# Softmax block factors of a perceiver layer: turned once a sequence and spread by DMA instead of widened and transposed for every block

## The chip, the cores and the metric

The kernel runs on one core of a Trainium2 chip. A core has five engines with a queue each: TensorE (PE, with its weight loads shown as PEld), VectorE (DVE), ScalarE (ACT), GpSimd (POOL) and SyncE (SP, which issues most DMAs here). Each queue is worked off in order, and engines wait for each other through semaphores. The metric is the device time of one execution in microseconds (us).

## The reference, cut to what matters

A layer of three parts over 16 sequences of 128 rows by 512 in float32: cross attention to a context of 2048 rows a sequence (16 heads of 32), a Mamba block with an MLP, and a gated expert layer. The change touches the attention's softmax and some instructions beside it:

```
q, k, v = heads(layernorm(x) @ wq.T + bq), heads(ctx @ wk.T + bk), heads(ctx @ wv.T + bv)
attn = softmax(q @ k.T * 32 ** -0.5)          # over 2048 columns of the context
x = x + (attn @ v) @ wo.T + bo
x_dbl = silu(conv(x_part)) @ x_proj_w.T       # 1024 -> 32 + 16 + 16 (dt, B, C)
dt = softplus(x_dbl[:32] @ dt_proj_w.T + b)   # then a scan over the rows
```

## The kernel before, in words

The context of a sequence is worked off in SB = 4 blocks of 512 rows. A block's softmax uses the block's own maxima; the four results are joined at the end with a factor for each row, block and head: the exponential of block maximum less overall maximum, over the joined sum. These factors are in `stats[b]`, 128 rows by 4 x 16.

The main loop runs over units u. In the first NU = 256 units, each does one group of four heads of one block: `scores` (L302) of the four heads into banks[0] to banks[3] of PSUM, `maxima` (L310, DVE), `exps` (L320, ACT), then four turns: turn i transposes columns i of all four heads' exponentials (L333) into a bank, and a copy to the tile pT frees it (L338 on ACT; L336 on DVE for turn 2, except in the first three units of a sequence, where ACT does all four). In the next unit `weighted` (L346) multiplies them with v. So a sequence b takes 16 units, from 16b on, and its end is called e = 16b + 16. Beside this, a unit holds

- the keys and values of the next blocks in a Strassen-like scheme of seven products (L240, into pa and pc), whose differences of context tiles t1 to t4 POOL makes (`ctx_sums`, L232) in every fourth unit, and whose sums are made on DVE and ACT (`k_sum` L260 and L258, `v_sum` L270 and L268),
- the Mamba part of earlier sequences, two at a time: `decays` (L665, ACT), `scan` (L679 and L682, DVE) and sums on POOL (`inputs` L644, ysum L695), from unit 54 on; `dt_third` (L632 to L635, POOL) makes dt and dx for four units each,
- and what the tables put in: functions are filed by unit under late, after, inner, middle, loads, head and behind, each table having a fixed place in the loop's body. `late` functions take a PSUM bank of their own; turn 3 then comes after them.

After NU the units hold the MLP and experts (`feed`) beside the remaining scans.

At the end of a sequence: `joined` (head of e) gathers the maxima (four copies, L422), `joined_first` (inner of e), `shares` and `joined_second` (e+1) and `joined_third` (head of e+2, L447) make the factors. `spread_out` (POOL, L453) repeats each factor over the 32 columns of its head in a tile fx. `scaled`, late in e+3 for block 0 and in e+4 for blocks 1 to 3, transposes fx with four transposes (L459) into a bank and multiplies the block's result avs by it, L464 for block 0 and L466 for the others, and POOL sums up (L467). `attended` (e+6, L472) takes the sum.

Further names: `turned` (L389, copy L391) transposes the normalized queries in unit 16b - 6; `x_proj` (L581, copy L584) is late in every unit 18 of 32, with a weight tile of 64 columns; `dt_first` (L611, L618), `dt_second` (L625) and `silu_second` (L570) are DVE and PE work of the Mamba part. SP issues the context tiles (L154), the rows B and C spread over all partitions (`load_bc`, L593) and weights.

Of the kernel before, what the change touches and what calls it, by code (L numbers as in the profile page):

```python
# [8 lines left out]
FP = mybir.dt.float32  # L9
AF = mybir.ActivationFunctionType  # L10
ALU = mybir.AluOpType
# [4 lines left out]
P = 128  # L16
B, NQ, D, S = 16, 128, 512, 2048
H, HD = 16, 32
KC = D // P
SB = S // 512  # L20
DI, DS, DTR = 1024, 16, 32
EC = DI // P
# [3 lines left out]
GT = GB * NQ  # L26
# [8 lines left out]
def perceiver_layer(ctx: ExitStack, tc: tile.TileContext, a: dict, out: bass.AP):  # L35
    nc = tc.nc
# [18 lines left out]
    x1d = dram.tile([B, NQ, D], FP, tag="x1d", name="x1d")  # L55
    zd = [dram.tile([NQ, D], FP, tag=f"zd{b}", name=f"zd{b}") for b in range(B)]
    xnd = [dram.tile([NQ, D], FP, tag=f"xnd{b}", name=f"xnd{b}") for b in range(B)]
    bcd = [dram.tile([2 * DS, GT], FP, tag=f"bcd{g}", name=f"bcd{g}") for g in range(B // GB)]

    mv = const.tile([P, B, 2], FP, tag="mv", name="mv")  # L60
# [48 lines left out]
    with ExitStack() as es:  # L109
# [8 lines left out]
        def acon_in(name, shape, src=None):  # L118
            t = acon.tile(shape, FP, tag=name, name=name)
            nc.gpsimd.dma_start(t, a[name] if src is None else src)  # L120
            return t
# [19 lines left out]
        def heads(ps):  # L141
            return ps.rearrange("p (k q) -> p k q", q=P)
# [171 lines left out]
        def exps(u):  # L314
            b, sb, hg = split(u)
            nm, sm = stats[b]
            pr = pool.tile([P, 4, 512], FP, tag="pr", name=f"pr{u}", bufs=1)
            for j in range(4):
                h = hg * 4 + j
                nc.scalar.activation(  # L320
                    pr[:, j, :],
                    banks[j],
                    AF.Exp,
                    bias=nm[j][:, sb, hg : hg + 1],
                    accum_out=sm[:, sb, h : h + 1],
                )
            prs[u] = pr
# [89 lines left out]
        def joined(b):  # L417

            parts, sm = stats[b]
            nm = keep.tile([P, SB, H], FP, tag="nm", name=f"nm{b}")  # L420
            for j in range(4):
                nc.vector.tensor_copy(  # L422
                    nm.rearrange("p s (k j) -> p s k j", j=4)[:, :, :, j], parts[j]
                )
            stats[b] = nm, sm
# [18 lines left out]
        def joined_third(b):  # L444
            nm, sm, lo, flat = stats[b]
            stats[b] = nm
            nc.vector.tensor_tensor(nm, nm, lo.to_broadcast([P, SB, H]), ALU.mult)  # L447

        fxs = {}

        def spread_out(b, sb):
            fx = keep.tile([P, H, HD], FP, tag="fx", name="fx", bufs=3)
            nc.gpsimd.tensor_copy(fx, stats[b][:, sb, :].unsqueeze(2).to_broadcast([P, H, HD]))  # L453
            fxs[b, sb] = fx.rearrange("p h d -> p (h d)")

        def scaled(b, sb, ps):
            fx = fxs.pop((b, sb))
            for hg in range(4):
                nc.tensor.transpose(heads(ps)[:, hg, :], fx[:, hg * P : (hg + 1) * P], ident)  # L459
            t = avs.pop((b, sb))  # L460
            if sb == 0:
                aT = keep.tile([P, KC, P], FP, tag="aT", name="aT", bufs=1)
                avs[b] = aT
                nc.vector.tensor_tensor(aT, t, heads(ps), ALU.mult)  # L464
            else:
                nc.vector.tensor_tensor(t, t, heads(ps), ALU.mult)  # L466
                nc.gpsimd.tensor_tensor(avs[b], avs[b], t, ALU.add)  # L467

        def out_proj(aT, b, ps):
# [10 lines left out]
            moments_of(b)  # L480


        xproj = acon_in("xproj", [P, EC, DTR + 2 * DS])
        convw = acon_in("convw", [P, EC, 4])
        convb = acon_in("convb", [P, EC])
        dtb = acon_in("dtb", [P, EC])
# [89 lines left out]
            sgs.clear()  # L576

        def x_proj(g, ps):
            ps = ps[0 : DTR + 2 * DS, 0:GT]
            for ec in range(EC):  # L580
                nc.tensor.matmul(  # L581
                    ps, xproj[:, ec, :], xas[g, ec], start=(ec == 0), stop=(ec == EC - 1)
                )
            nc.vector.tensor_copy(xd[0 : DTR + 2 * DS, :], ps)  # L584
            nc.sync.dma_start(bcd[g], xd[DTR : DTR + 2 * DS, :])

        def load_bc(t, base):

# [41 lines left out]
        def dt_third(g, ec):  # L630
            dt, e, u = dts[g, ec]
            nc.gpsimd.tensor_tensor(dt, dt, e, ALU.subtract)  # L632
            nc.gpsimd.tensor_tensor(dt, dt, u, ALU.add)
            dx = ssm.tile([P, GT], FP, tag="dx", name="dx")
            nc.gpsimd.tensor_tensor(dx, dt, xas[g, ec], ALU.mult)  # L635
            dts[g, ec] = dt, dx
# [111 lines left out]
        def flat(ps):  # L748
            return ps.rearrange("p k q -> p (k q)")
# [3 lines left out]
        def bank():  # L753
            return free_banks.pop(0)

        def give_back(*ps):
            free_banks.extend(ps)
# [379 lines left out]
            )  # L1137


        early = {}  # L1140
        late, after, inner, middle, loads, head, behind = ({} for _ in range(7))

        def put(where, u, f):
            where.setdefault(u, []).append(f)

        for b in range(B):
            s = 16 * b
            if b:
                put(loads, s - 8, lambda b=b: load_x(b))
                put(loads, s - 5, lambda b=b: load_w(0, b))  # L1150
                put(inner, s - 8, lambda b=b: moments_of(b))
                put(middle, s - 7, lambda b=b: root_of(b))
                put(inner, s - 7, lambda b=b: normal(b))
                put(late, s - 4, lambda ps, b=b: queries(b, ps))
            e = s + 16
            put(loads, e + 5, lambda b=b: load_w(3, b))
            put(head, e, lambda b=b: joined(b))
            put(inner, e, lambda b=b: joined_first(b))
            put(middle, e + 1, lambda b=b: shares(b))
            put(inner, e + 1, lambda b=b: joined_second(b))  # L1160
            put(head, e + 2, lambda b=b: joined_third(b))
            for sb in range(SB):
                put(inner, e + 2 + (sb > 0), lambda b=b, sb=sb: spread_out(b, sb))
                put(late, e + 3 + (sb > 0), lambda ps, b=b, sb=sb: scaled(b, sb, ps))
            put(late, e + 6, lambda ps, b=b: attended(b, ps))
            put(middle, e + 7, lambda b=b: root_of(b))
            put(inner, e + 7, lambda b=b: normed(b))
            put(late, e + 8, lambda ps, b=b: z_turned(b, ps))
        for g in range(NG):
            p = 32 * (g + 1)  # L1170
            for ec in range(EC):
                put(loads, p + 8 + ec, lambda g=g, ec=ec: load_win(g, ec))
                put(loads, p + 8 + ec, lambda g=g, ec=ec: load_win(g, EC + ec))
                put(late, p + 9 + ec, lambda ps, g=g, ec=ec: x_part(g, ec, ps))
                put(late, p + 9 + ec, lambda ps, g=g, ec=ec: z_part(g, ec, ps))
                put(after, p + 10 + ec, lambda g=g, ec=ec: silu_first(g, ec, xas))
                put(after, p + Z_GATES[ec], lambda g=g, ec=ec: silu_first(g, ec, zss))
            put(late, p + 18, lambda ps, g=g: x_proj(g, ps))
            s = p + LAG
            for ec in range(EC):  # L1180
                put(loads, s - 4 + 4 * ec, lambda ec=ec: load_dtproj(ec))
                put(behind, s - 3 + 4 * ec, lambda ps, g=g, ec=ec: dt_first(g, ec, ps))
                put(middle, s - 2 + 4 * ec, lambda g=g, ec=ec: dt_second(g, ec))
                put(inner, s - 2 + 4 * ec, lambda g=g, ec=ec: dt_third(g, ec))
            for i in range(GB):
                for ec in range(WS):
                    put(loads, s + 32 + 2 * i, lambda g=g, i=i, ec=ec: load_wout(g, i, ec))
                put(loads, s + 31 + 2 * i, lambda b=g * GB + i: reload_x(b))
                put(late, s + 33 + 2 * i, lambda ps, g=g, i=i: projected(g, i, ps))
# [68 lines left out]
        ps = banks[2]  # L1258
# [8 lines left out]
        for u in range(last):  # L1267
            live = u < NU
# [39 lines left out]
                x_products(of, made, phase, pa, pc)  # L1308
            if live:
                exps(u)  # L1310
            if makes and u % 4 == 1:
                ctx_sums(made, ("t1", "t2"))
            if 0 <= u + 1 - 32 - LAG < 32 * NG:
                inputs(*divmod(u + 1 - 32 - LAG, 32))
            if makes and u % 4 == 1:
                ctx_sums(made, ("t3", "t4"))
            silu_third()
            if scans:
# [12 lines left out]
            if live and after_turns:  # L1331
                if u % 4 == 0:
                    places = [flat(avp), *places[:-1]]
                elif u % 2 and makes and u not in behind:
                    places[-1] = flat(pc)
            taken = sum(any(p is b for b in banks) for p in places)
            if live:
                for i in range(3 if taken else 4):
# [103 lines left out]
```

## Time and profile before

| what | value |
|---|---|
| median of 3 runs | 3791.14 us (3790.33 to 3794.2) |
| the profiled execution | 3793.75 us, span 3792.0 us, granted clock 0.996 |
| L459, transposes of fx | 256 matmuls, median 273 ns each |
| L464, L466, products with the factors | 16 + 48, 673 to 687 ns |
| L453, the widened factors on POOL | 64, 599 to 621 ns |
| L581, x_proj | 128 matmul records, weight load of 64 columns 137 ns |
| bc to landing | 512 DMAs of 512 KB, median 4.3 us |

A matmul's duration is its latency; matmuls follow each other faster than that. Rows of the timeline give the start in us, the duration in us, the engine, the line, the operation, the tiles written and read, the shapes and the count merged in the row; in brackets stands the idle time before it and what ended it. A unit is measured from its first L302 to that of the next unit. The middle batches repeat themselves within some hundredths of a us, with a period of 32 units.

### The profile page before, as it was taken

What the parts mean: (1) busy time and instruction counts of PE and PEld (TensorE: products, weight loads), DVE (VectorE), ACT (ScalarE), POOL (GpSimd) and SP (SyncE); (2) the same over time, 40 slices, a digit from 0 to 9 for tenths busy, and PEclk for the clock granted to TensorE, in tenths of its full rate; (3) what the DMA queues carried; (4) which work ended last, traced back from release to release, by engine and by line L of the source; (5) the groups of instructions that cost most, each with busy time, mean ns of one, the idle gap of its engine ahead of it and who ended that gap; (6) DMA issues with size and microseconds to landing.
All of it is one profiled execution on the core that took longest, in us unless ns stands there. A gap on an engine that the chain in (4) does not pass through costs nothing.

```text
span 3792.0 us, 70325 instructions
## 1 busy us (share of the span) xinstructions
PE 3742.2 (99%) x26120; PEld 2853.8 (75%) x26120; DVE 2689.9 (71%) x4853; ACT 2443.5 (64%) x5848; POOL 2109.4 (56%) x1969
## 2 busy tenths in 40 slices
PE   9999999999999999999999999999999999999999
PEld 7878887778777877787788878787878776655555
DVE  3444445887778777877788778877887777778843
ACT  3555556777767776777677767776777675544421
POOL 2111213675657666765666566766675667667720
PEclk9999999999999999999999999999999999999999
DMA  3111122444444435453534453445444558577752
GB/s 102 34 40 43 49 72 80 132 149 145 141 159 145 154 117 174 136 159 111 184 130 145 131 191 119 148 134 171 140 156 132 165 174 290 197 276 246 266 174 73
DMA packets 343223, 548.40 MB, mean 145 GB/s; under 512 B 24368, under 2 KB 227408, under 8 KB 342624
## 3 DMA queue, kind: packets, MB, share of 16 engines
q1 hardware_dynamic: 342432, 543.27, 43.2%
q8 instruction: 206, 3.38, 0.4%
q14 instruction: 137, 1.12, 0.1%
q0 software_dynamic: 448, 0.63, 0.1%
HBM read 527.29 MB, written 16.52 MB: 143 GB/s over the span
## 4 chain that ended last, share of the span: by engine, by line
PE 89%; DVE 5%; ACT 3%; DMA 1%; issue 1%; POOL 1%; SPq 0%; DVEq 0%; POOLq 0%; ACTq 0%
PE pa L240 24%; PE pc L240 17%; PE bank L333 11%; PE bank L302 7%; PE avp L346 6%; PE bank L527 5%; PE bank L1029 2%; PE bank L934 2%; PE bank L472 2%; PE bank L708 2%; PE bank L903 1%; PE avp L399 1%; PE pc L708 1%; PE avp L934 1%; PE pa L934 1%
## 5 line engine op out<-in xcount | busy, mean ns | idle before, releaser
L310 DVE TENSOR_REDUCE nm<-bank 128x1 f32<-128x512 f32 x1024 | 635.2, 682 | 249.2 <-PE bank L302 249.0
L695 POOL TENSOR_TENSOR ysum<-ysum,w 128x512 f32<-128x512 f32 x384 | 500.0, 1302 | 481.9 <-DVE hst L658 312.7
L320 ACT ACTIVATE pr<-bank,nm 128x512 f32<-128x512 f32 x1024 | 689.7, 687 | 96.0 <-DVE nm L310 92.0
L644 POOL TENSOR_TENSOR w<-dx,bc 128x512 f32<-128x512 f32 x512 | 653.8, 1298 | 4.6
L679 DVE TENSOR_TENSOR_SCAN hst<-hst,w 128x512 f32<-128x512 f32 x459 | 560.7, 1222 | 15.8 <-ACT hst L665 9.3
L338 ACT COPY pT<-bank 128x512 f32<-128x512 f32 x816 | 434.8, 585 | 180.8 <-PE bank L333 177.1
L665 ACT ACTIVATE hst<-dt,alog 128x254 f32<-128x254 f32 x918 | 439.2, 478 | 148.5 <-DVE hst L658 133.0
L333 PE MATMUL bank<-ident,pr 128*128 128x128 f32 x4096 | 514.3, 274 | 7.2 <-ACT pT L338 3.3
L333 PEld LDWEIGHTS bank<-ident,pr 128*128 128x128 f32 x4096 | 469.6, 141 | 57.5 <-issue 13.8
L346 PEld LDWEIGHTS avp<-pT,v 128*32 128x32 f32 x8192 | 208.6, 110 | 194.6 <-issue 176.7
L682 DVE TENSOR_TENSOR w<-hst,bc 128x512 f32<-128x512 f32 x459 | 317.4, 692 | 26.0 <-DMA bc<-bcd 10.4
L232 POOL TENSOR_TENSOR t<-c,c 128x512 f32<-128x512 f32 x128 | 164.0, 1281 | 260.0 <-PE pc L240 255.9
L302 PE MATMUL bank<-kt,qT 32*128 32x512 f32 x2048 | 300.9, 642 | 0.5 <-ACT pT L338 0.5
L346 PE MATMUL avp<-pT,v 128*32 128x128 f32 x8192 | 277.6, 276 | 0.0
L240 PE MATMUL pa<-t,ks 128*128 128x256 f32 x1024 | 249.9, 387 | 6.2 <-POOL t L232 6.2
L240 PE MATMUL pa<-vs,t 128*128 128x256 f32 x1008 | 244.7, 386 | 0.0
L240 PEld LDWEIGHTS pa<-t,ks 128*128 128x128 f32 x1024 | 184.9, 190 | 44.2 <-issue 10.6
L240 PEld LDWEIGHTS pa<-vs,t 128*128 128x128 f32 x1008 | 185.5, 190 | 34.6 <-issue 10.1
L320 ACT ACTIVATION_READ_ACCUMULATOR pr<-bank,nm 128x1 f32 x1024 | 209.8, 205 | 0.0
L336 DVE COPY pT<-bank 128x512 f32<-128x512 f32 x208 | 143.7, 691 | 90.7 <-PE bank L333 89.4
L232 POOL TENSOR_TENSOR t<-c,t 128x512 f32<-128x512 f32 x128 | 163.3, 1276 | 36.1 <-issue 19.2
L527 PE MATMUL bank<-zT,win 128*128 128x256 f32 x800 | 183.1, 379 | 0.0
(325 smaller groups left out, 6884.9 us busy)
## 6 DMA issues: line engine op xcount, KB each, us to landing
bc<-bcd SPq DMA_DIRECT2D x512, 512.0 KB, 4.3
c<-in_ctxT_dram SPq DMA_DIRECT2D x256, 256.0 KB, 4.3
wf<-in_w_dram SPq DMA_DIRECT2D x124, 512.0 KB, 6.8
wqo<-in_wqkvo_dram SPq DMA_DIRECT2D x128, 256.0 KB, 4.6
win<-in_win_dram SPq DMA_DIRECT2D x128, 256.0 KB, 4.5
wout<-in_wout_dram SPq DMA_DIRECT2D x128, 256.0 KB, 4.1
x<-in_x_dram SPq DMA_DIRECT2D x16, 256.0 KB, 4.0
x1d<-x SPq DMA_DIRECT2D x16, 256.0 KB, 2.2
```

The costliest lines, as they stand in the source:

```text
L240: nc.tensor.matmul(ps[:, r, :], l[:, kc, r * P : (r + 1) * P], m[:, kc, :], start=(i in (1, 2, 5) and r == 0 and kc == 0), stop=(r == 1 an ...
L302: nc.tensor.matmul(banks[j], qts[b][rows, hg, :], kts[u // 4, hg][rows, :], start=True, stop=True)
L310: nc.vector.tensor_reduce(stats[b][0][j][:, sb, hg : hg + 1], banks[j], AX.X, ALU.max, negate=True)
L320: nc.scalar.activation(pr[:, j, :], banks[j], AF.Exp, bias=nm[j][:, sb, hg : hg + 1], accum_out=sm[:, sb, h : h + 1],)
L333: nc.tensor.transpose(ps[:, j, :], prs[u][:, j, i * P : (i + 1) * P], ident)
L338: nc.scalar.copy(pT, ps)
L346: nc.tensor.matmul(avp[j * HD : (j + 1) * HD, hg, :], vts[u // 4, hg // 2, i // 2][:, i % 2, hg % 2 * P + j * HD : hg % 2 * P + (j + 1) * HD],
L527: nc.tensor.matmul(ps, w[:, kc, :], zTs[g][:, kc, :], start=(kc == 0), stop=(kc == KC - 1))
L644: nc.gpsimd.tensor_tensor(w, dx.unsqueeze(1).to_broadcast([P, NH // 2, GT]), bcs[g * 32 + r, 0][:, i * NH // 2 : (i + 1) * NH // 2, :], AL ...
L665: nc.scalar.activation(bt(h[:, k, :])[:, :, 1:], bt(dt)[:, :, 1:], AF.Exp, scale=aneg[:, ec, n : n + 1],)
L679: nc.vector.tensor_tensor_scan(flat, flat, w.rearrange("p n t -> p (n t)"), 0.0, ALU.mult, ALU.add)
L695: nc.gpsimd.tensor_tensor(s, s, w, ALU.add)
```

## The change

The factors of a sequence (128 rows by 64) are now transposed once, in unit e+2 ahead of the turns, into banks[3]; ACT copies the 64 by 128 result to a tile shT, and SP writes it to DRAM. From there four DMAs a block, each to 32 partitions, spread it into fx in the layout that the product needs. So `spread_out` leaves POOL for SP (table loads, e+3 for blocks 0 to 2 in its place of the table and block 3 in e+4), the transposes of `scaled` go, and `scaled` itself moves from late to inner of the same units, with both inputs in SBUF.

Five more edits come with it: a single `turned` in its unit goes ahead of the turns, into banks[3]; `joined` moves from the head of e to inner of e-1; `ctx_sums` makes all four differences at once in units 5 of 16, ahead of `inputs`; `dt_third` moves from the end of a unit to the next unit, behind the first differences; and x_proj's weights are read 128 columns wide, from a tile padded with zeros at its end, of whose 128 result rows 64 are used.

```
+        def turned_shares(b, ps):
+            n = SB * H
+            nc.tensor.transpose(ps[0:n, 0:P], stats[b].rearrange("p s h -> p (s h)"), ident)
+            t = keep.tile([n, P], FP, tag="shT", name="shT", bufs=1)
+            nc.scalar.copy(t, ps[0:n, 0:P])
+            nc.sync.dma_start(shd[b], t)
         def spread_out(b, sb):
-            fx = keep.tile([P, H, HD], FP, tag="fx", name="fx", bufs=3)
-            nc.gpsimd.tensor_copy(fx, stats[b][:, sb, :].unsqueeze(2).to_broadcast([P, H, HD]))
-            fxs[b, sb] = fx.rearrange("p h d -> p (h d)")
+            fx = keep.tile([P, KC, P], FP, tag="fx", name="fx", bufs=3)
+            rows = shd[b].rearrange("(s k j) q -> s j k q", k=4, j=4)
+            for j in range(4):
+                nc.sync.dma_start(
+                    fx[j * HD : (j + 1) * HD], rows[sb, j].partition_broadcast(HD)
+                )
+            fxs[b, sb] = fx
-        def scaled(b, sb, ps):
+        def scaled(b, sb):
-            for hg in range(4):
-                nc.tensor.transpose(heads(ps)[:, hg, :], fx[:, hg * P : (hg + 1) * P], ident)
-                nc.vector.tensor_tensor(aT, t, heads(ps), ALU.mult)
+                nc.vector.tensor_tensor(aT, t, fx, ALU.mult)
-                nc.vector.tensor_tensor(t, t, heads(ps), ALU.mult)
+                nc.vector.tensor_tensor(t, t, fx, ALU.mult)
...
-            ps = ps[0 : DTR + 2 * DS, 0:GT]
+            ps = ps[:, 0:GT]
-                    ps, xproj[:, ec, :], xas[g, ec], start=(ec == 0), stop=(ec == EC - 1)
+                    ps,
+                    xproj[:, ec * NX : ec * NX + P],
+                    xas[g, ec],
...
-            put(head, e, lambda b=b: joined(b))
+            put(inner, e - 1, lambda b=b: joined(b))
+            put(first, e + 2, lambda ps, b=b: turned_shares(b, ps))
-                put(inner, e + 2 + (sb > 0), lambda b=b, sb=sb: spread_out(b, sb))
-                put(late, e + 3 + (sb > 0), lambda ps, b=b, sb=sb: scaled(b, sb, ps))
+                put(loads, e + 3 + (sb == 3), lambda b=b, sb=sb: spread_out(b, sb))
+                put(inner, e + 3 + (sb > 0), lambda b=b, sb=sb: scaled(b, sb))
-                put(inner, s - 2 + 4 * ec, lambda g=g, ec=ec: dt_third(g, ec))
+                put(between, s - 1 + 4 * ec, lambda g=g, ec=ec: dt_third(g, ec))
...
+            turns = ("t1", "t2", "t3", "t4") if u % 16 == 5 else ("t1", "t2")
             if makes and u % 4 == 1:
-                ctx_sums(made, ("t1", "t2"))
+                ctx_sums(made, turns)
+            for f in between.get(u, ()):
+                f()
...
-            if makes and u % 4 == 1:
+            if makes and u % 4 == 1 and len(turns) == 2:
                 ctx_sums(made, ("t3", "t4"))
...
+            if live and u % 16 == 10 and len(after_turns) == 1:
+                after_turns[0](banks[3])
+                after_turns, places = (), ()
+            for f in first.get(u, ()):
+                if live:
+                    f(banks[3])
```

## The prediction

> **What bounds the kernel now.** I read the page first, then the chain, then the timeline of single units, since an average says little about a loop whose units last 9 to 18 us.
>
> ```profile
> span 3792.0 us, 70325 instructions
> PE 3742.2 (99%) x26120; PEld 2853.8 (75%) x26120; DVE 2689.9 (71%) x4853; ACT 2443.5 (64%) x5848; POOL 2109.4 (56%) x1969
> PEclk9999999999999999999999999999999999999999
> PE 89%; DVE 5%; ACT 3%; DMA 1%; issue 1%; POOL 1%; SPq 0%; DVEq 0%; POOLq 0%; ACTq 0%
> ```
>
> TensorE (PE) is never idle at full clock, and 89% of the chain is its own. So a matmul taken away is a gain until another engine is late for PE. The question is who is late next. The timeline of units e+4 (from 1582.40) and e+5 (from 1595.03) of a middle batch answers it:
>
> ```profile
> 1582.07 0.68 DVE L464 TENSOR_TENSOR aT<-avs,bank 128x512 f32<-128x512 f32 x1
> 1582.40 1.53 PE L302 MATMUL bank<-kt,qT 32*128 32x512 f32 x8
> ...
> 1590.17 1.04 PE L459 MATMUL bank<-ident,fx 128*128 128x128 f32 x8
> ...
> 1592.63 1.45 POOL L695 TENSOR_TENSOR ysum<-ysum,w 128x512 f32<-128x512 f32 x1 [3.38 <-DVE hst L658]
> 1592.87 0.68 DVE L466 TENSOR_TENSOR avs<-avs,avp 128x512 f32<-128x512 f32 x1
> ...
> 1594.66 0.68 DVE L270 TENSOR_TENSOR v<-pc,u2vu 128x512 f32<-128x512 f32 x1
> 1595.03 1.14 PE L302 MATMUL bank<-kt,qT 32*128 32x512 f32 x8
> ...
> 1600.67 1.91 PE L333 MATMUL bank<-ident,pr 128*128 128x128 f32 x16
> ...
> 1603.09 2.00 PE L240 MATMUL pa<-t,ks 128*128 128x256 f32 x8 [0.51 <-POOL t L232]
> ```
>
> See here: a removed transpose is worth 0.109 us, not its 0.273 us duration (eight take 1.04). The scores of e+4 take 1.53 instead of 1.14, as one bank is still being read by L464: 0.39. The products of e+5 start 0.68 after the last transpose and not 0.11: with a second short wait 0.79 for the POOL differences. And DVE is just in time: L270, which makes the last piece of v, ends at 1595.34, and the weighted sum that reads it starts at 1596.1.
>
> **The transposes that go.** L459 runs 256 times. In e+3 four go (0.44), in e+4 twelve (1.31). With the bank wait, PE reaches the scores of e+5 2.14 us earlier, at 1592.89. With the 0.79 this would be 2.93 a batch.
>
> **What DVE does with it.** The products L464 and L466 now read two SBUF tiles; before, one operand was in PSUM. Two rows:
>
> ```profile
> L466 DVE TENSOR_TENSOR avs<-avs,bank x33: 673/681/683, 255.4 to 3149.8; 128x512 f32<-128x512 f32 x33
> ...
> L969 DVE TENSOR_TENSOR xr<-xr,x x14: 691/692/1649, 3182.3 to 3699.1; 128x512 f32<-128x512 f32 x14
> ```
>
> With a PSUM operand the duration never varies; from SBUF alone the same operation takes 0.69 or up to 1.65. The long ones end 0.55 after a POOL operation does: L969 at 3374.51 lasts 1.10, and L632 on POOL, which had waited during L966, holds it until 3375.06. They take turns. The Trainium skill ("SBUF — State Buffer", Who interferes with whom) states the rule that speaks against this change: a DVE instruction with two SBUF inputs and a GpSimd instruction that reads SBUF exclude each other for the whole instruction. The trace agrees. Without the rule DVE fits (0.60 a product, no loss) and I would forecast 2.93 x 12 = 35 us from these batches; with it, step by step, PE being 0.8 earlier in e+4 than before. In e+3 the first product ends near 1583.95 behind POOL's L695, so the maxima of e+4 begin 0.4 later than before (1583.55); ACT's exponentials stand behind the copy of avs (L360), which ends near 1584.75 by then, and lose nothing. In e+4 L682 ends 1591.75, L695 on POOL starts at once and ends 1593.3, product one ends 1593.85, two 1594.45; POOL's first sum (L467, 1.27) has waited and runs to 1595.65; product three ends 1596.2, L270 1596.8. The second half of PE's weighted sum, due at 1594.5, waits for L270 until 1596.9. Its rest (0.5) and the x products (3.56) put the transposes at 1600.9 (before 1600.67). DVE's maxima, behind L570 and POOL's second sum, begin at 1597.65; the fourth head's transpose follows maxima by 3.54 us in the unit at 1345 (1348.34 to 1351.88), so 1601.2: the same limit. Both say that 2.37 of the lead is lost. By then POOL has t1 and t2 (its sums end near 1598.7, plus two of 1.27), so the 0.79 is kept. Net gain **0.55 a batch**. It holds for the batches whose units e+2 to e+5 have scans beside them (scans begin in unit 54): 3 to 14, twelve, so 6.6 us.
>
> **What is added in e+2.** One transpose with 64 columns goes to banks[3] before the turns, and ACT's copy shT frees that bank. In ACT's order this copy stands behind the decays and L673, just ahead of the pT copies:
>
> ```profile
> 1566.98 1.91 PE L333 MATMUL bank<-ident,pr 128*128 128x128 f32 x16
> ...
> 1568.78 0.49 ACT L673 ACTIVATE xa<-xa,dskip 128x256 f32<-128x256 f32 x1
> 1569.18 2.02 ACT L338 COPY pT<-bank 128x512 f32<-128x512 f32 x4
> ...
> 1376.62 3.67 PE L581 MATMUL bank<-xa,xproj 128*64 128x256 f32 x16
> 1377.15 0.49 ACT L673 ACTIVATE xa<-xa,dskip 128x256 f32<-128x256 f32 x1
> 1377.55 1.53 ACT L338 COPY pT<-bank 128x512 f32<-128x512 f32 x3
> ```
>
> Turn 3 writes bank 3 too. It started at 1566.98 + 12 x 0.109 = 1568.29. Now shT starts at 1569.18 and takes 0.27 (0.585 for 512 columns, 0.372 for 256, carried on to 128), and with 0.1 for the signal turn 3 starts at 1569.55: +1.26. In every second batch x_proj stands there, also in bank 3: 1376.62 becomes 1377.92, +1.30. Its wider weights give 0.29 back: 64 columns lose 0.10 on entry, 0.13 inside (3.59 to the next transpose for 16 x 0.216) and 0.06 behind. So 6 x 1.26 + 6 x 1.01 = **13.6 us lost**. Nothing else covers this: PE's queue is in order, and behind turn 3 stand the y products and the next scores.
>
> By the skill ("TensorE: Matmul & The Clock Gate", LDWEIGHTS) a load takes time by its columns: L581's 137 ns would become L527's 190, and 53 ns x 128 would cost 6.8 us. But matmuls of both lines start 0.216 apart, so the longer load hides behind the matmul; I take the row.
>
> **The rest.**
> - Batches 0 to 2 have no scans, ACT and DVE have room, and batch 15 falls into the FFN stage: 16 x 0.109 gained, 0.31 paid for the narrow transpose (0.11 and 0.2 of changeover as at L581; 0.11 to 0.5 are its bounds): -1.43 each, -5.7.
> - x_proj of two groups without that wait: -0.6.
> - L389 alone in its unit moves ahead of the turns. Turn 3 waited for ACT's pT copy (0.40 idle, 0.06 slower). Now it waits for L391, behind L260 on DVE, by some 0.1: -0.4 in six units, -2.4.
> - joined moves ahead of the next unit's maxima. In every second unit e (the one at 1345.65) its four copies took 1.49 (the longest 1.25, behind POOL) and held the fourth exponential: 0.31 on PE. In the new place, ahead of L570, DVE stood idle 1.16 for ACT: -0.31 x 6, -1.9; in the other batches nothing.
> - dt_third comes behind t1 and t2 (all four in e+5). There L633 ends near 1605.2 (1598.7, four differences of 1.25, two additions of 0.75) and the decays of e+6, which head ACT's queue before the exponentials, ask about 1605.0. These 0.2 lie inside the slack of the exponentials (in e+5 before, 1596.19 + 3.54 against 1601.0: 1.3). inputs stands behind it: its first w ends 2.0 later, 1607.2, and the scan asks after the maxima, 1607.9. Bounds 0 to 0.6 a batch; I take 0. POOL loses 64 copies of 0.61, not on the path.
> - SP gets 16 writes and 256 spreads (0.34 each to issue), in slots without weight loads. The first four: shT at 1569.5, the write landing in 1.5 (as bcd), four issues, 4.3 to land (as bc): 1577.1, needed at 1582.5. Beside x_proj the bcd write stands ahead on SP; 1388 against 1394. The fourth block's spread waits on DVE for product one's buffer (1584), lands by 1590, needed at 1594.5. Queued behind it are bc for e+5 (needed 1599.85) and the next context tiles. So nothing; if a landing took 5 us more it would cost what is over.
>
> Sum: -6.6 + 13.6 - 5.7 - 0.6 - 2.4 - 1.9 = **-3.6 us**. The profiled execution took 3793.75 (span 3792.0 and 1.75 around it), 2.6 above the median of the three runs; on the median, 3791.14 - 3.6 = 3787.5.
>
> **Rivals.**
> *The lock bites less* (0.15): product three goes ahead of POOL's sum, or nothing blocks. Against: L966, L632, L969 took turns. Gain per batch 1.9 to 2.9: 3771 to 3759.
> *Bank 3 is free in time* (0.08): shT costs no PE time. For: one small copy. Against: ACT reached its first pT only at 1569.18. Without the 1.26 and 1.30 but with the 0.31: 13.6 becomes 2.0, 3776.
> *The lock bites more, and the kernel is slower* (0.27): in e+4 POOL gets in before product two as well, or the products are slowed in e+3 so that exponentials of e+4 are late. L270 comes 1.28 later and PE waits for it directly: gain 0.55 becomes a loss of 0.73, 12 x 1.28 = 15.4 more, 3803. It is slower than before once a batch gains under 0.25, that is when L270 ends over 0.3 later than my 1596.8; slower by 0.2% from 0.95 later. For it: the 0.3 is little.
> That the transposes stay is ruled out: the changed program's order on PE has none of L459's and one 64-column transpose a batch.
>
> **How the numbers follow.** 0.2% is 7.6 us, about what a measurement of this kernel can tell from no change. The likeliest case has 0.50, its own range 3778 to 3798 from +-0.5 in each of the two twelve-fold terms. Faster: 0.14 from the lighter lock, 0.07 from the free bank, 0.05 from the likeliest's edge: 0.26. Slower: 0.23 from the heavier lock, 0.07 from the edge: 0.30. Within: 0.44. The range leaves out the lock-free end and the far end of the heavy one: 3767 to 3808.
>
> **What would show it.** L464's and L466's successors at mean 1.1 or more, varying; PE waiting for DVE v or ACT pr in e+5; turn 3 or x_proj waiting about 1 us for ACT shT in e+2; no wait of L302 on L466 and none of L240 on POOL t; from scores to scores, units e+3 to e+5 together 32.15 instead of 32.70, and e+2 at 12.24 and 15.69 instead of 10.98 and 14.68. Products steady at 0.69, or no wait on shT, would prove me wrong.

## The result and the profile after

The changed kernel takes 3809.48 us (median, 3807.33 to 3811.03) against 3791.49 (3790.33 to 3794.2): ratio 1.0047, 95% interval 1.0036 to 1.0059. It is 18 us slower where 3.6 less were forecast, and just outside the range. PE has 240 matmuls fewer and is busy 23.4 us less (3742.2 before) in a span that is 17.3 longer, so some 40 us of new idle time has to be found, and busy time at a lower clock beside it. The page after, its span, engines and chain:

```profile
span 3809.3 us, 70241 instructions
...
PE 3718.8 (98%) x25880; PEld 2835.3 (74%) x25880; DVE 2749.0 (72%) x4854; ACT 2444.8 (64%) x5864; POOL 2092.3 (55%) x1905
...
PE 85%; DVE 9%; ACT 3%; issue 2%; DMA 1%; POOL 1%; SPq 0%; DVEq 0%; ACTq 0%; POOLq 0%
```

DVE holds 9% of the chain instead of 5%. Since the loop is periodic, I compared unit by unit, from scores to scores. The profiled spans differ by 17.3: the stretch up to unit 64 is 6.1 shorter, units 64 to 254 are 10.9 longer (2343.9 to 2354.8), and from the scores of unit 255 to the end it takes 12.5 more (693.8 to 706.3). In the middle part all units are equal to 0.05 except these (in the batches with scans):

| unit | before | after | forecast |
|---|---|---|---|
| e+2 | 10.98 | 12.30 | 12.24 |
| e+2 with x_proj | 14.68 | 15.64 | 15.69 |
| e+3 | 10.08 | 9.64 | 9.64 |
| e+4 | 12.63 | 10.93 | |
| e+5, in 7 of 12 batches | 9.99 | 11.54 | |
| e+5, in 5 of 12 | 9.99 | 13.23 | |
| e+3 to e+5 together | 32.70 | 32.11 or 33.80 | 32.15 |
| 16 (mod 32) | 14.70 | 14.39 | 14.39 |
| 26 (mod 32), most | 12.00 | 11.48 | 11.6 |

So nearly every step of the middle part came out as worked out. Two things did not: five of the long e+5, and the tail.

**e+4 and e+5.** The timeline of the same batch as in the prediction (e+4 from 1581.22), first DVE, then POOL, then PE:

```profile
1591.31 4.03 DVE L478 TENSOR_TENSOR avs<-avs,fx 128x512 f32<-128x512 f32 x3
1595.27 0.68 DVE L271 TENSOR_TENSOR v<-pc,u2vu 128x512 f32<-128x512 f32 x1
...
1596.67 2.47 DVE L311 TENSOR_REDUCE nm<-bank 128x1 f32<-128x512 f32 x4
```

```profile
1591.07 1.45 POOL L715 TENSOR_TENSOR ysum<-ysum,w 128x512 f32<-128x512 f32 x1 [2.20 <-DVE hst L678]
1593.14 4.73 POOL L479 TENSOR_TENSOR aT<-aT,avs 128x512 f32<-128x512 f32 x3 [0.63 <-DVE avs L478]
1597.84 1.26 POOL L233 TENSOR_TENSOR t<-c,c 128x512 f32<-128x512 f32 x1
```

```profile
1581.22 1.14 PE L303 MATMUL bank<-kt,qT 32*128 32x512 f32 x8
...
1592.16 1.14 PE L303 MATMUL bank<-kt,qT 32*128 32x512 f32 x8
1593.23 0.65 PE L347 MATMUL avp<-pT,v 128*32 128x128 f32 x16
1596.00 0.64 PE L347 MATMUL avp<-pT,v 128*32 128x128 f32 x16 [2.12 <-DVE v L271]
```

Compare this with the lines of before. The scores of e+4 are back at 1.14 and PE reaches e+5 early. DVE's three products last 1.76, 0.68 and 1.75 (three by 0.68 before), the long ones beside POOL's L715 and its first L479. L271, in order behind them, ends at 1595.95, and PE stands 2.12 us in the middle of its weighted sum. All this had been forecast. What had not is what comes behind the wait in five batches. Windows of 3.4 us in such a batch (first three rows) and in another (last two); after the length, the busy time of PE, PEld, DVE, ACT and POOL, then the granted TensorE clock, DMA share and GB/s:

```profile
1403.60:1407.00 3.40, 1.28 (x30) 0.78 (x23) 3.40 (x5) 0.16 (x1) 3.24 (x3) 1.00 0.86 239
1407.00:1410.40 3.40, 3.40 (x10) 2.68 (x9) 3.37 (x6) 3.00 (x10) 3.32 (x3) 0.50 0.62 245
1410.40:1413.80 3.40, 3.40 (x26) 3.15 (x24) 2.02 (x5) 2.62 (x7) 3.32 (x5) 1.00 0.00 0
1198.80:1202.20 3.40, 1.67 (x21) 1.37 (x22) 3.40 (x5) 0.28 (x1) 3.24 (x3) 1.00 0.96 330
1202.20:1205.60 3.40, 3.40 (x22) 3.04 (x21) 3.31 (x5) 3.29 (x10) 3.32 (x4) 1.00 0.11 44
```

The clock is granted anew on a fixed grid of 3.41 us: every stretch of halved clock in these traces that ends before the kernel does lasts 3.41, 6.83 or 10.24. In the first batch the whole wait falls into one window, PE is busy 38% of it, and the next window is granted half the clock: the same products take 3.42 for eight instead of 1.99. In the other batch the grid cuts the wait, the window is busy 49%, and nothing follows. Of this trace's windows at full clock, those with PE busy up to 43% were followed by half clock, and those at 49% or more were not. A wait of 2.12 lies wholly within one window of 3.41 in a bit over a third of all positions (an estimate, 1.29 / 3.41); five of twelve batches were hit (from 806, 1407, 1803, 2387 and 2987 us). In the kernel before, the clock is never halved between 55 us and the FFN stage. The Trainium skill ("TensorE: Matmul & The Clock Gate", The HAM clock gate) states this grid of 3413 ns, and half clock after a window of idleness. Here a window was enough in which PE stood idle for 57 to 62%.

**The tail.** The FFN stage after the change, PE's, DVE's and SP's timelines in turn:

```profile
3154.50 1.12 PE L954 MATMUL pa<-wf,hs 128*128 128x512 f32 x2 [1.36 <-DMA wf<-in_w_dram]
...
3169.66 1.09 PE L894 MATMUL avp<-ident,xr 128*128 128x128 f32 x4 [8.02 <-DVE xr L820]
```

```profile
3144.81 0.69 DVE L702 TENSOR_TENSOR w<-hst,bc 128x512 f32<-128x512 f32 x1 [2.12 <-DMA bc<-bcd]
...
3156.99 0.69 DVE L702 TENSOR_TENSOR w<-hst,bc 128x512 f32<-128x512 f32 x1 [4.99 <-DMA bc<-bcd]
...
3160.13 4.02 DVE L478 TENSOR_TENSOR avs<-avs,fx 128x512 f32<-128x512 f32 x3
...
3168.45 2.74 DVE L820 SCALAR_TENSOR_TENSOR xr<-xr,rz,normw 128x512 f32<-128x512 f32 x2
```

```profile
3139.29 0.50 SPq L458 DMA_DIRECT2D shd<-shT  x1
3140.20 0.79 SPq L613 DMA_DIRECT2D bc<-bcd  x1
3144.93 5.55 SPq L465 DMA_DIRECT2D fx<-shd  x12
3150.58 0.85 SPq L791 DMA_DIRECT2D wf<-in_w_dram  x2
3151.52 0.86 SPq L613 DMA_DIRECT2D bc<-bcd  x2
```

The same place in the kernel before, DVE and then PE:

```profile
3138.51 0.69 DVE L682 TENSOR_TENSOR w<-hst,bc 128x512 f32<-128x512 f32 x1 [4.86 <-DMA bc<-bcd]
...
3144.88 0.69 DVE L682 TENSOR_TENSOR w<-hst,bc 128x512 f32<-128x512 f32 x1 [1.35 <-DMA bc<-bcd]
...
3148.64 1.87 DVE L466 TENSOR_TENSOR avs<-avs,bank 128x512 f32<-128x512 f32 x3
...
3154.26 1.93 DVE L800 SCALAR_TENSOR_TENSOR xr<-xr,rz,normw 128x512 f32<-128x512 f32 x2
```

```profile
3156.25 0.66 PE L874 MATMUL bank<-ident,xr 128*128 128x128 f32 x4 [0.44 <-DVE xr L800]
```

Read the lines after the change from SP's up. The write of shd lands after 5.6 us (1.8 in the median of all sixteen), while bc and other tiles of 256 to 512 KB are on their way. SP stands for it until 3144.93, then issues twelve spreads for 5.55, and only then the wf and bc tiles that others need next. DVE stood for bc before as well (4.86 and 1.35), but now the second of these w products waits 4.99 and starts 54.0 after the start of unit 255 instead of 46.7: 7.3 later. Behind it, in order, stand the three products (4.02 beside POOL's sums, 1.87 before) and z_norm (L820), by then 9.4 later. PE comes to the transposes of z_norm and stands 8.02, where its matmuls had stood 0.44 before. Within that wait, at 3164.9, the clock is halved for 10.2 us; 5.5 of these lie behind the wait, where PE works at half speed and loses some 2.7 (an estimate, half of 5.5).

**e+2**, the wait for shT, as forecast (PE, then ACT):

```profile
1565.05 1.47 PE L334 MATMUL bank<-ident,pr 128*128 128x128 f32 x12
1567.54 0.66 PE L334 MATMUL bank<-ident,pr 128*128 128x128 f32 x4 [1.02 <-ACT shT L457]
```

```profile
1566.85 0.49 ACT L693 ACTIVATE xa<-xa,dskip 128x256 f32<-128x256 f32 x1
1567.24 0.24 ACT L457 COPY shT<-bank 64x128 f32<-64x128 f32 x1
```

### The profile page after: what moved, and what is told of

It is laid out like the page before. It is cut to its first block, busy times and chain, and to the rows that moved or that the text cites. A ratio compares the mean times of both kernels' runs of the same rounds, so it can differ in the third digit from the quotient of the medians.

```text
span 3809.3 us, 70241 instructions
## 1 busy us (share of the span) xinstructions
PE 3718.8 (98%) x25880; PEld 2835.3 (74%) x25880; DVE 2749.0 (72%) x4854; ACT 2444.8 (64%) x5864; POOL 2092.3 (55%) x1905
## 4 chain that ended last, share of the span: by engine, by line
PE 85%; DVE 9%; ACT 3%; issue 2%; DMA 1%; POOL 1%; SPq 0%; DVEq 0%; ACTq 0%; POOLq 0%
PE pa L241 22%; PE pc L241 16%; PE bank L334 11%; PE bank L303 6%; PE avp L347 6%; PE bank L543 4%; PE bank L923 2%; PE bank L1049 2%; PE bank L954 2%; DVE nm L311 2%; DVE hst L699 2%; PE bank L484 2%; PE bank L728 2%; PE avp L400 1%; DVE w L702 1%
## 5 line engine op out<-in xcount | busy, mean ns | idle before, releaser
L715 POOL TENSOR_TENSOR ysum<-ysum,w 128x512 f32<-128x512 f32 x384 | 500.2, 1303 | 485.7 <-DVE hst L678 293.1
```

The source lines that it names most:

```text
L715: nc.gpsimd.tensor_tensor(s, s, w, ALU.add)
```

## The experiments

All start from the changed kernel, and each was timed beside runs of the kernel before on its chip (medians 3792.2 to 3792.7).

**e1 and e5: PE kept busy in the wait, to test the clock.**

```diff
                         stop=(i == 3),
                     )
+                if i == 1 and u % 16 == 4 and 64 < u < NU - 8:
+                    busywork(u + 1)      # e1: r in 8 steps, e5: r in 3 steps
...
+            for r in (0, 1, 0, 1, 0, 1, 0, 1):
+                nc.tensor.matmul(pa[:, r, :], w[:, 0, 0:P], x[:, 0, :], start=True, stop=True, ...)
```

> The changed kernel with eight matmuls (0.216 us each, into pa, overwritten at once by the x products) between the first and the second half of the weighted sum in units e+5, where PE stands 2.1 us for DVE's v in all twelve batches with scans. Clock theory: the wait itself stays, but a window of 3.41 us with PE busy under some 45% no longer occurs there, so the five half-clock stretches near 806, 1407, 1803, 2387 and 2987 us are gone: 5 x 1.68 = 8.4 us less than the changed kernel, some 3801. Rival, the five long units come from contention (DMA or weight loads slowed by SBUF traffic): they stay long, 3809 or a little more.

> As e1_filler with three products instead of eight: the sixteen matmuls of e1 took 3.66 us and outlasted the wait, six take about 1.4 and end before DVE's v is there. Clock theory: e+5 lasts 11.54 in all twelve batches, none of its windows is half-clock, and the time is 8.4 us less than the changed kernel's 3809.5, some 3801. Rival, the five long units have another cause: they come back, 3809.

e1: 3820.06, ratio 1.0073 [1.0061, 1.0086]. Each step is two matmuls on PE, so sixteen took 3.66 us, outlasted the wait, and e+5 lasts 13.00 in all twelve batches. Slower, but none of the five half-clock stretches is there. e5, with six: 3803.43, ratio 1.0028 [1.0017, 1.0038]. e+5 lasts 11.54 in all twelve batches; units 64 to 254 are 8.1 shorter than in the changed kernel (worked out: 5 x 1.68 = 8.4). The window with the wait in e5, and the next:

```profile
802.90:806.30 3.40, 2.76 (x39) 1.86 (x40) 3.40 (x5) 0.43 (x1) 3.24 (x3) 1.00 0.95 302
806.30:809.70 3.40, 3.40 (x16) 2.97 (x17) 3.40 (x6) 2.71 (x9) 3.32 (x3) 1.00 0.37 147
```

In the changed kernel this second window had 0.50. In e5 idle work makes the kernel faster, and in both runs all twelve batches are free of the halved clock: the five long units are the clock's. The rival, contention, falls. e1's 3801 was missed, since its filler was twice as long as meant.

**e2: POOL's sums a unit later.**

```diff
-                nc.gpsimd.tensor_tensor(avs[b], avs[b], t, ALU.add)
+                avs[b, sb, "s"] = t          # added by POOL at the end of e+5
...
+                if sb:
+                    put(inner, e + 5, lambda b=b, sb=sb: added(b, sb))
```

> The changed kernel with POOL's three sums (L479) moved from e+4 behind the products to the end of e+5. Lock theory: the third product no longer waits for POOL's first sum and takes 0.68 instead of 1.75; L271 ends 1.07 earlier, PE's wait in the weighted sum falls from 2.1 to about 1.06, and the windows there stay over 45% busy, so no half-clock stretch: 12 x 1.07 + 8.4 = 21 us less, some 3788. Rival, the products are slow for what they read and not for POOL: the third stays at 1.7 and the time at 3809. Rival two, turns of e+5 then wait for the exponentials: only the 8.4 and a part of the 12.8 come, 3795 to 3801.

3850.35, ratio 1.0149 [1.0133, 1.0164]: a clear miss. POOL's queue and DVE's in that place:

```profile
1205.64 1.72 POOL L233 TENSOR_TENSOR t<-c,c 128x512 f32<-128x512 f32 x1
1207.44 1.59 POOL L233 TENSOR_TENSOR t<-c,t 128x512 f32<-128x512 f32 x1
1208.99 1.71 POOL L233 TENSOR_TENSOR t<-c,c 128x512 f32<-128x512 f32 x1
```

```profile
1204.47 5.11 DVE L478 TENSOR_TENSOR avs<-avs,fx 128x512 f32<-128x512 f32 x3
1209.50 0.68 DVE L271 TENSOR_TENSOR v<-pc,u2vu 128x512 f32<-128x512 f32 x1
```

With its sums out of the way POOL goes straight on to the differences of e+5, which are ready and also read SBUF. Now all three products alternate with POOL (1.76, 1.76, 1.74), and POOL's own 1.27 become up to 1.72. L271 is 1.1 later instead of earlier, e+5 lasts 12.6 to 15.4, and e+6 waits for aT besides. That the two engines exclude each other is confirmed, from the other side: what mattered in the changed kernel was that POOL had nothing ready during the second product, because its sums depended on DVE. That second product reads the same kinds of tiles and lasts 0.68, so the rival, that the products are slow for what they read, falls. My expectation moved one POOL operation away and forgot the one behind it.

**e3 and e7: batch 15.**

```diff
+            if b < B - 1:
                 put(first, e + 2, lambda ps, b=b: turned_shares(b, ps))
+                if b == B - 1:               # e3: POOL copies and transposes, as before
+                    put(inner, e + 2 + (sb > 0), ... spread_old(b, sb))
+                    put(late, e + 3 + (sb > 0), ... scaled_old(b, sb, ps))
...
+                if b == B - 1:               # e7 instead: all a little later
+                    put(inner, e + 4 + (sb > 0), ... scaled(b, sb))
+                    put(inner, e + 3 + (sb > 1), ... spread_out(b, sb))
```

> The changed kernel with batch 15 alone done as in the kernel before (factors copied by POOL, transposed by PE into PSUM; no write, no spread). Theory: the 12.5 us lost behind the start of unit 255 come from SP's queue, which stands for the landing of shd and then issues twelve spreads ahead of the bc tiles that the scan waits for; with these gone they come back: some 3797. Rival, the tail is lost to the other edits (dt_third and the first products moved, the wide x_proj) or to the shifted start of the FFN units: it stays, 3806 or more.

> The changed kernel with batch 15's spreads issued at the end of units e+3 and e+4 and its products a unit later, so that SP doesn't stand for the landing of shd ahead of the bc tiles; the products still read two SBUF tiles. SP theory: most of the 11 us that e3_b15_old won come back as well, 3799 to 3803. Rival, the tail is lost to the products' lock with POOL in the FFN units, or to the 12 issues themselves: it stays at 3808 to 3812.

e3: 3800.64, ratio 1.0023 [1.0014, 1.0032]; from unit 255 to the end it takes 695.3 instead of 706.3, 11.0 less, with units 64 to 254 unchanged to 0.1. So 11.0 of the tail's 12.5 go with batch 15's new way. The other 1.5 stay, and the side edits alone (e6, below) have a tail of 696.4, 2.6 longer than before. e7: 3804.86, ratio 1.0033 [1.002, 1.0045], tail 703.1, between its two expectations. Its PE timeline:

```profile
3157.18 0.63 PE L894 MATMUL avp<-ident,xr 128*128 128x128 f32 x4 [0.62 <-DVE xr L820]
3158.86 0.63 PE L894 MATMUL bank<-ident,xr 128*128 128x128 f32 x4 [1.05 <-DVE xr L820]
3171.41 5.40 PE L484 MATMUL bank<-wqo,aT 128*128 128x512 f32 x8 [5.06 <-POOL aT L479]
```

With the spreads behind the bc tiles and the products a unit later, the wait of 8.02 falls to 0.62, but the output projection now waits 5.06 for aT. The w product that waited 4.99 starts 48.3 after the start of unit 255 here (54.0 in the changed kernel, 46.7 before). So 5.7 of z_norm's 9.4 come from the spreads that stand ahead of bc on SP and from SP's wait before them; 1.6 stay even here, and 2.1 come from the products and what follows them on DVE. How the 5.7 divide between SP's standing for the landing and its twelve issues was not separated.

**e4: the narrow transpose elsewhere.**

```diff
-                    f(banks[3])
+                    f(avp[:, 3, :])
```

> The changed kernel with the narrow transpose of the shares into the part of avp that the fourth head group will use, instead of banks[3]. Bank theory: turn 3, or x_proj, no longer waits for ACT's shT copy: e+2 loses its 1.24 and 1.04 us stalls, 6 x 1.24 + 6 x 1.04 = 13.7 us less, some 3796, give or take two half-clock stretches of 1.7 that fall or don't as the windows shift. Rival, the turns are late because the shT copy delays ACT's own pT copies: at most 2 us less.

3793.35, ratio 1.0005 [0.9996, 1.0013]; 16.1 less than the changed kernel. e+2 falls from 12.30 to 11.11 and from 15.64 to 14.50: 6 x 1.19 + 6 x 1.14 = 14.0, and four half-clock stretches fell into the middle part instead of five (1.7). ACT's order is as it was:

```profile
1559.44 0.49 ACT L693 ACTIVATE xa<-xa,dskip 128x256 f32<-128x256 f32 x1
1559.85 0.24 ACT L457 COPY shT<-avp 64x128 f32<-64x128 f32 x1
```

So the bank, not ACT's order, was the price.

**e6: the side edits alone.** All batches as batch 15 in e3.

> The changed kernel with the factors of all batches the old way (POOL copies, sixteen transposes, products with PSUM): what is left of the change are the side edits (joined a unit earlier, the single late matmul first, t1 to t4 and dt_third reordered, x_proj 128 wide). By the prediction's terms: 1.9 (unit 16) + 2.4 (unit 26) + 0.6 for the wide x_proj in eight groups + up to 0.68 x 12 = 8 for POOL's differences being there in e+5: some 13 less than before, 3779. Rival, the old factor copies on POOL push the differences as late as before: 5 less, 3787.

3779.9, ratio 0.9965 [0.9953, 0.9978], about as worked out, but in part by chance: units 64 to 254 are 15.0 shorter than before, and the tail is 2.6 longer. e+5 lasts 9.21 instead of 9.99: POOL's differences are there in time. Unit 16 has its 0.31, unit 26 its 0.43 in the mean, and e+2 with x_proj is 0.29 shorter, as forecast for the wider weights. e+2 without x_proj rose by 0.13 in five batches, which was not traced. The turned factors, then, cost what is between: 29.6 us. They cost something in e+3 to e+5 too: these three units last 31.92 here, and 32.11 in the changed kernel even where the clock stays full. The gain of 0.59 against the kernel before is the side edits' 0.78 less 0.19.

**e8, e9, e10: where the products can go.** With e4's place and e3's batch 15.

```diff
-                put(inner, e + 3 + (sb > 0), lambda b=b, sb=sb: scaled(b, sb))
+                put(inner, e + (3, 4, 4, 5)[sb], ... scaled(b, sb))                        # e8
+                put(between if sb == 3 else inner, e + (3, 4, 4, 5)[sb], ... scaled(b, sb))  # e9
+                put((ahead, ahead, ahead, inner)[sb], e + (3, 3, 4, 4)[sb], ... prod(b, sb))  # e10, on POOL
```

> The changed kernel with the narrow transpose in avp (as e4), batch 15 the old way (as e3), and the fourth product with its sum moved from e+4 to the end of e+5. Theory: 3809.5 - 16 - 9 = 3784 from the first two; from the third L271 ends 1.67 earlier, PE's wait in the weighted sum falls from 2.1 to about 0.5, no window there falls to half clock (8.4 less) and 0.9 to 1.6 of each batch's lead is kept (11 to 19 less): 3757 to 3765. Rival, the fourth product in e+5 meets POOL's work there and delays k's sums or the maxima of e+6 by as much: 3775 or more.

> As e8_fixed, but the fourth product and its sum stand behind the maxima of e+5 and ahead of dt_third (in e8 the sum came behind dt_third and more on POOL, and the output projection of e+6 waited 4.5 us for aT). Theory: e+5 keeps its 9.9 and e+6 falls from 20.6 or more to about 14.4: 12 x 6.5 = 78 us less than e8's 3835, and the half-clock stretches behind that wait go: 3752 to 3765. Rival, the product behind the maxima meets POOL's differences, lasts 1.7 and delays k's sums, so that PE waits in e+5: e+5 at 11 to 12, 3770 to 3785.

> As e8_fixed, but all four products and the three sums on POOL (1.27 each): two products ahead of the turns of e+3, the third and the first sum ahead of the turns of e+4, the rest at the end of e+4. Theory: DVE has no product of two SBUF tiles left there, so L271 is on time, PE doesn't wait in the weighted sum, no half-clock stretch; e+5 at 9.2 to 9.6: 3809.5 - 16 - 9 - 8.4 - 12 x 2.1 = 3751. Rival, POOL's work now blocks DVE's scans and w products in e+3 and e+4 and its own L715 comes late: these units grow by 1 us or more each, 3775 or more.

e8: 3835.0, ratio 1.0111 [1.0095, 1.0126], far above the 3757 to 3765 expected. e+5 falls to 9.87, the 1.67 worked out, but e+6 rises to 20.4 to 21.9, since the last sum stands behind other work on POOL, and the halved clock follows:

```profile
1031.09 5.40 PE L496 MATMUL bank<-wqo,aT 128*128 128x512 f32 x8 [4.22 <-POOL aT L491]
```

e9: 3764.99, ratio 0.9931 [0.9918, 0.9945], the upper end of what was expected: e+5 keeps 9.87, e+6 is at 15.02 and not 14.4. e10: 3750.48, ratio 0.9891 [0.9877, 0.9904], the fastest: e+5 is at 9.21 and e+3 to e+5 gain 2.91 a batch, the 2.93 that the prediction had without the lock. Its POOL, DVE and PE:

```profile
987.48 1.27 POOL L488 TENSOR_TENSOR avs<-avs,fx 128x512 f32<-128x512 f32 x1
```

```profile
987.02 1.22 DVE L723 TENSOR_TENSOR_SCAN hst<-hst,w 128x512 f32<-128x512 f32 x1
988.28 0.69 DVE L726 TENSOR_TENSOR w<-hst,bc 128x512 f32<-128x512 f32 x1
...
998.99 0.68 DVE L271 TENSOR_TENSOR v<-pc,u2vu 128x512 f32<-128x512 f32 x1
```

```profile
999.84 1.14 PE L303 MATMUL bank<-kt,qT 32*128 32x512 f32 x8
1000.91 1.08 PE L347 MATMUL avp<-pT,v 128*32 128x128 f32 x32
```

L271 ends before the scores of e+5, the weighted sum runs through in one piece, and neither e9 nor e10 has a half-clock stretch between 51 us and the FFN stage. POOL takes four products of 1.27 a batch where the kernel before had four copies of 0.61, and e+3 and e+4 stay at 9.64 and 10.93.

## Why the prediction was wrong

Two steps failed. The forecast of -3.6 was 20.9 below the 17.3 that the profiled executions differ by. The term of batch 15 accounts for 13.9 of this (12.5 + 1.4), the clock behind PE's wait for 8.4; what remains, 1.4, goes the other way and lies mostly in the start of the two executions.

- **Batch 15: wrong, and the larger part.** "Batch 15 falls into the FFN stage" gave -1.43, by the count of transposes alone. The tail took 12.5 more, 11.0 of it with batch 15's new way (e3). The step on SP ended in "So nothing", from units of the middle part, where the shd write lands in 1.8, and added that a landing 5 us later would cost what is over. In the FFN units it was 3.8 later, with wf and bc tiles queued behind on SP. No unit of that stage had been read for it.
- **The transposes that go, and the lock: right, but its wait was priced too low.** L476 and L478 last 1.34 in the mean (forecast 1.1 or more), the last piece of v is there 14.7 after the start of e+4 (forecast 14.8), POOL's differences no longer hold PE. The net gain was put at 0.55 a batch; it was 0.59 in seven batches. In the other five it was a loss of 1.10. The step that failed is "waits for L270 until 1596.9" (L271 in the changed kernel): a wait of 2.4 was written down there (2.12 measured), and its price taken as its length. Behind it the clock was halved for 3.41 us, 1.68 more each, 8.4 in all (e1, e5). The rival "The lock bites more" had the right side and the wrong cause: L271 was not late. And the 0.79 for POOL's differences belongs to the side edits: e6 keeps all transposes and has it too.
- **e+2: right.** 13.6 forecast, 6 x 1.32 + 6 x 0.96 = 13.7 measured, and the bank shown by e4.
- **The narrow transpose:** 0.31 where nothing waits was too much; units 18 and 34 grew by 0.11. Units e+2 to e+5 of batches 0 to 2 gained 5.2, where 4.3 stood. The whole stretch up to unit 64 gained 6.1, of which 1.8 is unit 1 alone: there the halved clock of the start lay in the profiled execution of before (12.52) and not in that after (10.74). It is not the change's.
- **The side edits: right in the middle part.** Unit 16 gave -1.9 and unit 26 some -2.5 as forecast, the wide x_proj 0.29 a group (e6). For dt_third 0 was taken; e+6 grew by 0.05 in seven batches, but not in e6, where dt_third stands in the same place. In e6's tail 2.6 were lost, half of it in the wait that stays open below; neither was forecast.

The sum again, for units 64 to 254: 13.7 for e+2, 12 x -0.59 = -7.1, 8.4 for the clock, -1.9 and some -2.5 for units 16 and 26, 0.3 for e+6: 10.9, as measured. With -6.1 before and 12.5 behind, 17.3.

Open: PE's wait for wf at unit 257 was 2.5 before, 3.9 in the changed kernel and 2.7 in e3. It does not follow batch 15's spreads: e6, which has none, has 3.8, and e10, with batch 15 the old way, 4.1. So about 1 us of e3's 11.0 may be this wait and not the new way; what sets it was not traced.

## What to carry to other kernels

Price an idle stretch of PE by its length and by what it leaves of the clock's window: here 2.1 us within 3.41 cost 1.7 more in the batches where they fell together, and idle work in it took that away. When an operand moves from PSUM to SBUF, look for what the neighbour engine has ready at that moment, and for the operation behind it too; where two engines only take turns, try the work on the one with room (e10). And walk a periodic change through its last period separately: there the queues hold other work, and a transfer that mostly lands in 1.8 us can hold up all that is queued behind it.

## What was not expected of the hardware

- The halved clock needs no window that is idle throughout: in the changed kernel's trace windows at full clock with PE busy 38 to 43% of 3.41 us were followed by one at 0.50, those from 49% up were not. Over all twelve traces windows between 42 and 54% went either way, by the traces' modelled matmul ends. As the grid doesn't follow the program, the same wait is hit in some batches only, and e3, e4 and e7 with the same wait had five, four and four.
- The alternation of DVE and POOL shows where DVE reads two SBUF tiles: in e10 POOL's products of 1.27 run beside DVE's scans (1.22) and w products (0.69), whose state lies in PSUM, and neither gets longer.
